# Local attention and whitening on one core: second sums, bias, first band transposes and one weight buffer moved, and the conv weights' loads on another queue

## The chip, the cores and the metric

The kernel runs on one core of one Trainium2 chip. The metric is the device time of one execution in microseconds (us). The engines carry the names that the profile gives them: PE multiplies matrices (PEld is its weight load), DVE does elementwise work and 32x32 block transposes, ACT does activations, scaled copies and copies out of PE's result memory, POOL is GpSimd, and SP issues DMAs. Each engine works through its own list in order. DMAs issued by SP travel on the hardware-driven queue (q1 in the profile), those issued by POOL on the software-driven one (q0).

## The reference, cut to what matters

The input has 4 images of 256 channels and 64 x 64 pixels, in fp32. Two layers follow each other:

```python
# layer 0: attention weights from a dilated 7x7 convolution, then a weighted sum of 49 shifts
k = conv(x, w1, padding=6, dilation=2) + b1          # 256 -> 128 channels, 7 x 7
k = conv(k, w2) + b2                                 # 128 -> 49 channels, 1 x 1
attn = softmax(k, axis=1)
x = einsum('bkchw,bkhw->bchw', the 49 shifts of x by two pixels, attn)
# layer 1: whitening in four groups of 64 channels, by 5 Newton-Schulz steps
mean, Sigma = mean and covariance (+1e-5 I) of each group over all images and pixels
Sigma_N = Sigma / trace(Sigma);  P = I
for _ in range(5): P = 1.5 * P - 0.5 * (P @ P @ P) @ Sigma_N
out = (P / sqrt(trace(Sigma))) @ (x - mean) * weight + bias
```

The statistics of layer 1 need the whole output of layer 0, so all four images go through the attention before the first output is written.

## The kernel before

**The convolution.** The two convolutions are folded into one from 256 channels to 49 (lines 177 to 247). Because of the dilation by two, the four pixel phases of an image are separate small images, and the kernel computes their 7 x 7 convolution by an evaluate, multiply and interpolate scheme in both directions. There are seven evaluation points (EVAL), of which the rows 1 to 5 and the columns 1 to 5 are combinations with small factors; point 0 and the point INF at infinity read the image directly. For one image and one row point `br`, `row_eval` (L437) makes the row's combination on DVE in one of three buffers `rb`; `col_ops` (L471) makes from it the column points `xh`; `conv_bank` (L518) multiplies them with the transformed weights on PE in three banks (BANKS: points 1, 2, 0, then 3, 4, INF, then 5), 96, 80 and 32 profiled matmuls of 0.275 us, and copies each bank to `pv` on ACT (L546); `col_interp` (L615) interpolates on DVE into `zz`. After the last row `row_interp` (L641) interpolates over the rows and adds the bias on ACT (L658), which gives the logits. Image 0 takes rows 1, 2 and 3 like this, and its rows 0, 4, 5 and INF by direct sums on PE (`direct`, L662, 56 profiled matmuls, 11.6 us); images 1 to 3 take rows 0 to 5 by `conv_bank` and INF by a direct sum.

A direct sum for a row that carries two weight rows comes in two parts. The part `s == 0` is copied to `zz`. The part `s == 1` is one row lower; its last row is copied on ACT (L690) and the rest is added on DVE (L691).

**The weights.** `weights` (L364) makes the transformed weights of one row and bank the first time that they are wanted, on DVE with copies and scalings on ACT or POOL, stores them in memory (`gd`, L434), and loads them from there for each later image (L378), 45 loads in all: 588, 490 and 196 KB for the banks 0, 1 and 2. Each bank has one buffer (tags wr0 to wr2), so a load waits until the matmuls of the same bank of the row before have read it. Rows 4 and 5 have their row combination parked in memory (`kept`); it is loaded for image 1 into `rb[0]` (L387), from which that row's weights are then made.

**The attention.** `softmax(b, pc)` (L849) works on one column parity: PE turns the logits (L859), DVE takes the maximum (L865), ACT the exponentials (L873), DVE scales (L886). An attention block n = 4b + 2h + pc then goes through memory: `move_terms` (L895) copies its terms to `zt` (L919) and stores them to `sd` (L932); `load_band` (L952) reads them back as a banded matrix in three parts, each with four DMAs (L960), and transposes each part in place on DVE (L973). `make_block` (L985) turns the image on PE, `weighted_sum` (L1009) multiplies it with the band (L1020), `store_y` (L1030) writes the result over the image (ACT L1039), and `turn_y` and `moments` gather the covariance (L1052, L1060, L1073).

**Memory.** Five image slots stand for eight half images. Images 1 and the first half of image 2 are loaded by `load_x` (L126) on POOL's queue; later `move` (L1086) spills a finished slot to memory (L1091) and loads the next half image into it (two DMAs of 1 MB, L130), also on POOL.

**The order.** `conv_step` (L719) runs one bank and at once prepares the same bank of the next row. Blocks of attention of the image before are put between the steps by a plan with eight gaps per image (L1171 to L1226). PE's instructions keep the order of the program (`pe`). On the other engines and on the queues a scheduler orders instructions when the program is built, by priority and by when it takes them to be ready. `tc.high_priority()` raises a priority; `add_manual_dep` with NoSync fixes an order without a wait; `in_turn` and `in_order` chain DVE's instructions strictly, throughout image 0's convolution and around the last rows of the others. `later` is a list of final copies that are put behind the ACT copy of the next bank 1 (L550 to L560).

Of the kernel before, what the change touches and what calls it, by code (L numbers as in the profile page):

```python
# [10 lines left out]
AF = mybir.ActivationFunctionType  # L11
# [21 lines left out]
def kernel(  # L33
# [330 lines left out]
    def weights(b, br, i, mid=None):  # L364

        first = (br, i) not in made  # L370
        made.add((br, i))
        s0 = slot_of[BANKS[i][0]]
        ns = sum(len(taps(bc)) for bc in BANKS[i])
        nk = NSK * len(taps(br)) // 2
        wt = apool.tile([P, ns, NSK], F32, tag=f"wr{i}", name=f"wr_{b}_{br}_{i}")[:, :, :nk]
        w = {bc: wt[:, slot_of[bc] - s0 : slot_of[bc] - s0 + len(taps(bc))] for bc in BANKS[i]}
        if not first:
            nc.sync.dma_start(wt, gd[br][:, s0 : s0 + ns])  # L378
            return w

        if br == 0:
            g = [gr0[:, v] for v in range(KS)]
        elif br in kept:

            f = rb[0].rearrange("p q r c w -> p (q r c w)")[:, : KS * nk]
            if i == 0:
                nc.sync.dma_start(f, kept[br])  # L387
            f = f.rearrange("p (v a r k) -> p v a r k", v=KS, a=NCC, k=KT)
            g = [f[:, v] for v in range(KS)]
        else:  # L390
            g = [gbr[:, v] for v in range(KS)]
        g = [t.rearrange("p a r k -> p (a r k)") for t in g]

        e = ct.rearrange("p a b -> p (a b)") if b else store[4].rearrange("p c r w -> p (c r w)")
        e, o, e1 = (e[:, k * nk : (k + 1) * nk] for k in range(3))
        g0 = [g[KS - 1 - a] for a in range(4)]
        g1 = [g[KS - 5 - a] for a in range(3)]
        o0 = {bc: w[bc][:, 0] for bc in w}
        o1 = {bc: w[bc][:, 1] for bc in w if bc != INF}

        same = nc.scalar.copy if b == 0 else nc.gpsimd.tensor_copy
        if i == 0:
            add(e, g0[0], g0[2])
            add(o, g0[1], g0[3])
            add(e1, g1[0], g1[2])
            add(o0[1], e, o)
            sub(o0[2], e, o)
            add(o1[1], e1, g1[1])
            sub(o1[2], e1, g1[1])
            same(o0[0], g0[0])  # L410
            same(o1[0], g1[0])
        elif i == 1:
            madd(e, g0[2], 4.0, g0[0])
            madd(o, g0[3], 4.0, g0[1])
            madd(e1, g1[2], 4.0, g1[0])
            madd(o0[3], o, 2.0, e)
            madd(o0[4], o, -2.0, e)
            madd(o1[3], g1[1], 2.0, e1)
            madd(o1[4], g1[1], -2.0, e1)
            same(o0[INF], g0[3])  # L420
        else:
            madd(o0[5], g0[0], 2.0, g0[1])
            madd(o1[5], g1[0], 4.0, g1[2])
            madd(o0[5], o0[5], 2.0, g0[2])
            if mid is not None:
                mid()
            madd(o1[5], g1[1], 2.0, o1[5])
            madd(o0[5], o0[5], 2.0, g0[3])
            add(o1[5], o1[5], o1[5])
        for bc in BANKS[i]:  # L430
            f = SCALE[bc] * (SCALE[br] if br not in kept else 1.0)
            if f != 1.0:
                nc.scalar.mul(w[bc], w[bc], f)
        nc.sync.dma_start(gd[br][:, s0 : s0 + ns], wt)  # L434
        return w
# [205 lines left out]
    def row_interp(b, part):  # L641

        pt = {k: zz[:K2, k] for k in range(NP)}
        lg = lgx
        if b == 0:
            lg = store[4].rearrange("p c r w -> p (c r w)")
        lg = lg[:, : SH * W].rearrange("p (r w) -> p r w", w=W)
        outs = phases(lg[:K2])
        cut = lambda t, k: t[:, k : k + Q8]
        tr = ct.rearrange("p a b -> p (a b)")[:K2, : Q9 * W].rearrange("p (q w) -> p q w", w=W)  # L650
        interpolate(pt, tr, outs, cut, part)
        if part == 0:
            done_ = ((0, outs[0]), (2, outs[2]))
        else:
            done_ = ((3, cut(pt[5], 0)), (1, outs[1]))
            logits[b] = lg
        for a, t in done_:
            nc.scalar.activation(outs[a], t, AF.Identity, bias=bias[:K2])  # L658

    logits = {}  # L660

    def direct(b, br, s, ps, w, xr=None):  # L662


        a = 3 if br == INF else 0
        order = [(v, cc) for v in sorted(range(KS), key=lambda v: abs(v - R)) for cc in range(NCC)]
        for j, (v, cc) in enumerate(order):
            d = 2 * (v - R)
            w0, w1_ = max(0, -d), min(W, W - d)
            for h in range(2):  # L670
                if xr is None:
                    xs = slots[2 * b + h].rearrange("p c (q a) w -> p a q c w", a=4)[:, a]
                else:
                    xs = xr[:, :, h]
                pe(
                    nc.tensor.matmul(  # L676
                        ps[h * HB : h * HB + KT, :, w0:w1_],
                        w[v][:, cc],
                        xs[:, :, cc, w0 + d : w1_ + d],
                        start=(j == 0),  # L680
                        stop=(j == len(order) - 1),
                        skip_group_check=True,
                    )
                )
        z = zz[:K2, br]
        if s == 0:
            with tc.high_priority():
                nc.scalar.copy(z[:, :Q8], ps[:K2])
        else:
            nc.scalar.copy(z[:, Q8], ps[:K2, Q8 - 1])  # L690
            add(z[:, 1:Q8], z[:, 1:Q8], ps[:K2, : Q8 - 1])  # L691

    def conv_psum():
        ncv[0] += 1
# [102 lines left out]
    for i in three:  # L797
        bank(2, i)
    row_weights(4)
    keep_weights(4)  # L800
    xrs[4] = row_eval(0, 4)
    direct0(4, 0)
# [46 lines left out]
    def softmax(b, pc):  # L849

        lv = logits[b].rearrange("p r w -> p (r w)")
        nm = f"{b}_{pc}"
        mx = work.tile([P, NCH, 2], F32, tag="mx", name=f"mx_{nm}")
        lt = []
        for hf in range(2):
            lt.append(tp().rearrange("p (i h k) -> p i h k", i=NI, h=2))
            for i in range(NI):
                pe(
                    nc.tensor.transpose(  # L859
                        lt[hf][:, i].rearrange("p h k -> p (h k)")[:, :K2],  # L860
                        lv[:K2, bass.ds(2 * (NI * hf + i) * P + pc, P, 2)],
                        ident[:K2, :K2],
                    )
                )
            nc.vector.tensor_reduce(  # L865
                mx[:, NI * hf : NI * (hf + 1)], lt[hf][:, :, :, :KT], AX.X, ALU.max
            )
        nc.vector.tensor_scalar(mx, mx, -1.0, None, ALU.mult)  # L868
        d = terms[b, pc] = bpool.tile([P, 2, NCH, KT], F32, tag="d", name=f"d_{nm}", bufs=2)
        s = work.tile([P, 2, NCH], F32, tag="s", name=f"s_{nm}")  # L870
        for h in range(2):
            for i in range(NCH):
                nc.scalar.activation(  # L873
                    d[:, h, i], lt[i // NI][:, i % NI, h, :KT], AF.Exp,
                    bias=mx[:, i, h : h + 1], accum_out=s[:, h, i : i + 1],
                )
            nc.vector.reciprocal(s[:, h], s[:, h])
            rm = work.tile([P, NCH, KS], F32, tag="rm", name=f"rm_{nm}_{h}")
            nc.vector.tensor_tensor(
                rm,  # L880
                s[:, h].unsqueeze(2).to_broadcast([P, NCH, KS]),
                cmask.unsqueeze(1).to_broadcast([P, NCH, KS]),
                ALU.mult,
            )
            dh = d[:, h].rearrange("p i (u v) -> p i u v", u=KS)
            nc.vector.tensor_tensor(  # L886
                dh, dh, rm.unsqueeze(2).to_broadcast([P, NCH, KS, KS]), ALU.mult
            )

    terms, moved, loaded = {}, set(), set()  # L890

# [57 lines left out]

    BAND = ((0, 3), (3, 5), (5, 8))  # L950

    def load_band(n, part):  # L952

        if (n, part) in loaded or n not in moved:
# [4 lines left out]
        for g in range(CR):  # L959
# [6 lines left out]
                ),  # L966
            )

        f = band.rearrange("p m r w -> p (m r) w")[
            :, m0 * BP + (R if m0 == 0 else 0) : m1 * BP - (R if m1 == NCH else 0)  # L970
        ].rearrange("p e w -> p (e w)")
        with tc.high_priority():
            nc.vector.transpose(f, f)  # L973
        if (n, part) == (4 * B - 1, len(BAND) - 1):
            bring_back(dma)

# [199 lines left out]

    def soft(b, pc):
        with tc.high_priority() if pc == 0 else nullcontext():
            softmax(b, pc)
        soft_done.add((b, pc))  # L1180
        if pc == 0:
            bands(4 * b)
# [263 lines left out]
```

## Time and profile before

| | us |
|---|---|
| median of 3 runs | 752.98 (752.46 to 753.97) |
| the profiled execution's time | 753.07 |
| its span, first to last instruction | 751.3 |
| DVE idle in the span (751.3 less 611.5 busy) | 139.8 |
| PE matmuls of the banks (L536), 4368 | 249.7 |
| PE matmuls of the weighted sums (L1020), 640 | 154.6 |
| SP's queue waiting at the weights' loads (L378) for PE | 135.9, in 26 waits |
| SP's queue waiting at the band loads (L960) for PE y | 69.9, in 22 waits |
| POOL waiting at the spills (L1091) for ACT | 127.3, in 3 waits |

The mean granted PE clock is 0.984. The chain that ended last is made of 60% PE, 27% DVE, 5% ACT, 4% DMA and 3% issue. Roughly, the span has the folding of the weights until 29 us, image 0's convolution until 157, image 1's with the attention of image 0 beside it until 300, the same for images 2 and 3 until 578, the rest of the attention until 682, the whitening matrices until 698, and the output.

How to read it: busy time is an engine's own; time in which an engine waits costs only where the others wait for it in turn. In a timeline a line gives start, duration, engine, source line, operation, what is written and read, the number of merged instructions, and in brackets the idle time before it and what ended it. L313, L306 and L309 are helpers (multiply-add, add, subtract), so their lines are told apart by tile names. In the windows' view the columns are the stretch, its length, the busy time and number of instructions of PE, PEld, DVE, ACT and POOL, then the granted PE clock, the DMA share and GB/s.

### The profile page before, as it was taken

Reading aid. Unit: us, or ns where it says so; the run is one execution under the profiler, and the core shown is the slowest. Engines: PE = TensorE matmul, PEld = TensorE weight load, DVE = VectorE, ACT = ScalarE, POOL = GpSimd, SP = SyncE. Lnnn points to the kernel's source line nnn. Section 1 sums busy time; section 2 is a strip of 40 time slices with the busy share of each in tenths; the row PEclk is TensorE's granted clock in tenths of the full one; section 3 lists DMA queues with packets and bytes.
Section 4 is the critical chain, followed back from the end, with each engine's and each line's share of the span. In section 5 each row is a group of like instructions: output and inputs, shape, how many; then the busy total and the mean of one; then the engine's idle time right before and its main releaser. Section 6 shows DMA issues by size and latency. Waiting matters only on the chain.

```text
span 751.3 us, 18491 instructions
## 1 busy us (share of the span) xinstructions
PE 706.7 (94%) x7512; PEld 531.5 (71%) x7512; DVE 611.5 (81%) x1268; ACT 332.3 (44%) x953; POOL 50.9 (7%) x52
## 2 busy tenths in 40 slices
PE   6999999997988997999999999999999889998996
PEld 1449643376887795599998976899998678885331
DVE  3799899998999988877997799799969665545575
ACT  1424240253564354375453443745435573322564
POOL 0410070020000110001000100000000000000000
PEclk9999999999999998999999999999999999999999
DMA  8981120127153393046743930433532243362588
GB/s 322 257 302 73 60 88 17 64 98 232 64 183 120 103 342 97 21 132 217 256 130 116 336 82 1 146 111 110 166 90 82 50 135 111 117 251 118 209 359 327
DMA packets 59629, 114.41 MB, mean 152 GB/s; under 512 B 22887, under 2 KB 42008, under 8 KB 58776
## 3 DMA queue, kind: packets, MB, share of 16 engines
q1 hardware_dynamic: 55848, 94.36, 37.7%
q0 software_dynamic: 3696, 18.88, 7.3%
q8 instruction: 59, 0.97, 0.5%
q14 instruction: 26, 0.21, 0.1%
HBM read 65.88 MB, written 47.33 MB: 151 GB/s over the span
## 4 chain that ended last, share of the span: by engine, by line
PE 60%; DVE 27%; ACT 5%; DMA 4%; issue 3%; SPq 1%; DVEq 0%; ACTq 0%
PE cv L536 18%; PE y L1020 13%; PE acc L676 6%; PE tp L1386 4%; PE sig L1073 3%; PE tp L1052 3%; PE cv L676 3%; PE tp L991 3%; DVE xh L313 3%; DVE pv L313 2%; DVE rb L313 2%; DVE zz L313 2%; DMA band<-sd 2%; DVE band L973 2%; PE cv L222 2%
## 5 line engine op out<-in xcount | busy, mean ns | idle before, releaser
L536 PE MATMUL cv<-xh,wr 128*49 128x128 f32 x4368 | 249.7, 275 | 5.9 <-DVE xh L306 5.6
L536 PEld LDWEIGHTS cv<-xh,wr 128*49 128x49 f32 x4368 | 243.6, 124 | 9.9 <-issue 7.1
L1020 PE MATMUL y<-band,xb 128*128 128x224 f32 (+2 forms) x640 | 154.6, 381 | 8.7 <-ACT xb L999 6.7
L1020 PEld LDWEIGHTS y<-band,xb 128*128 128x128 f32 x640 | 111.4, 196 | 31.4 <-ACT xb L999 9.4
L546 ACT COPY pv<-cv 113x486 f32<-113x486 f32 (+1 forms) x63 | 30.0, 476 | 84.6 <-PE cv L536 84.4
L1039 ACT ACTIVATE slot<-y,pivot 128x512 f32<-128x512 f32 x53 | 36.7, 740 | 67.5 <-PE y L1020 67.4
L1060 ACT COPY yt<-tp 128x256 f32<-128x256 f32 x128 | 45.5, 379 | 37.8 <-PE tp L1052 36.4
L973 DVE STREAM_TRANSPOSE band<-band 128x864 f32<-128x864 f32 (+1 forms) x48 | 47.6, 992 | 13.2 <-DMA band<-sd 13.1
L991 PE MATMUL tp<-ident,slot 128*128 128x128 f32 x256 | 50.0, 297 | 8.2 <-ACT yt L1060 8.2
L313 DVE SCALAR_TENSOR_TENSOR pv<-pv 113x162 f32<-113x162 f32 x186 | 55.2, 320 | 0.8 <-ACT pv L546 0.3
L1052 PE MATMUL tp<-ident,slot 128*128 128x128 f32 x256 | 52.0, 299 | 3.7 <-ACT yt L1060 1.0
L1052 PEld LDWEIGHTS tp<-ident,slot 128*128 128x128 f32 x256 | 41.2, 205 | 13.8 <-issue 4.0
L991 PEld LDWEIGHTS tp<-ident,slot 128*128 128x128 f32 x256 | 40.1, 205 | 14.8 <-ACT yt L1060 9.7
L873 ACT ACTIVATE d<-tp,mx 128x49 f32<-128x49 f32 x128 | 36.9, 337 | 21.4 <-DVE mx L868 17.9
L919 ACT COPY zt<-d 32x112 f32<-32x112 f32 (+2 forms) x156 | 44.8, 287 | 1.9
L313 DVE SCALAR_TENSOR_TENSOR xh<-ct 128x512 f32<-128x512 f32 x42 | 27.9, 685 | 13.7 <-PE cv L536 13.4
L1073 PEld LDWEIGHTS sig<-yt 128*64 128x64 f32 x1024 | 33.2, 140 | 6.4 <-issue 4.9
L1073 PE MATMUL sig<-yt 128*64 128x65 f32 x1024 | 37.7, 228 | 0.0
L999 ACT COPY xb<-tp 128x256 f32<-128x256 f32 x87 | 30.5, 375 | 14.0 <-PE tp L991 13.4
L999 DVE COPY xb<-tp 128x256 f32<-128x256 f32 x41 | 16.4, 421 | 23.4 <-PE tp L991 23.4
L676 PE MATMUL acc<-slot,tap 128*49 128x496 f32 (+3 forms) x168 | 34.6, 569 | 0.0
L873 ACT ACTIVATION_READ_ACCUMULATOR d<-tp,mx 128x1 f32 x128 | 30.8, 242 | 0.0
(222 smaller groups left out, 958.0 us busy)
## 6 DMA issues: line engine op xcount, KB each, us to landing
out_dram<-out SPq DMA_DIRECT2D x32, 512.0 KB, 3.4
sd<-zt SPq DMA_DIRECT2D x16, 896.0 KB, 4.0
slot<-in_x_dram POOLq DMA_DIRECT2D x12, 1024.0 KB, 10.1
band<-sd SPq DMA_DIRECT2D x128, 84.0 KB, 2.1
wr<-gd SPq DMA_DIRECT2D x15, 588.0 KB, 3.7
wr<-gd SPq DMA_DIRECT2D x15, 490.0 KB, 4.0
spill<-slot POOLq DMA_DIRECT2D x3, 2048.0 KB, 7.7
back<-spill SPq DMA_DIRECT2D x3, 2048.0 KB, 13.1
```

The costliest lines, as they stand in the source:

```text
L313: return in_turn(STT(o, a, f, b, ALU.mult, ALU.add))
L536: nc.tensor.matmul(cv[h * HB : h * HB + KT, k, sr : sr + n, sc : sc + n], wv[:, sc, sr, cc], xh[bc][:, :n, h * NCC + cc, :n], start=(j == ...
L676: nc.tensor.matmul(ps[h * HB : h * HB + KT, :, w0:w1_], w[v][:, cc], xs[:, :, cc, w0 + d : w1_ + d], start=(j == 0), stop=(j == len(order) ...
L873: nc.scalar.activation(d[:, h, i], lt[i // NI][:, i % NI, h, :KT], AF.Exp, bias=mx[:, i, h : h + 1], accum_out=s[:, h, i : i + 1],)
L919: ins = nc.scalar.copy(o, i)
L973: nc.vector.transpose(f, f)
L991: nc.tensor.transpose(t[:, cc * P : (cc + 1) * P], xt[:, cc, CR * m : CR * (m + 1), bass.ds(pc, SW, 2)], ident,)
L999: (nc.vector.tensor_copy if tail else nc.scalar.copy)(xb, t[:, :C])
L1020: nc.tensor.matmul(ps[:, cc, q0 - half * HALF : q1 - half * HALF, :], xb[:, cc * P : (cc + 1) * P], rhs, start=(k == 0), stop=(k == len(PI ...
L1052: nc.tensor.transpose(t[:, cc * P : (cc + 1) * P], yt[:, cc, CR * i : CR * (i + 1), bass.ds(pc, SW, 2)], ident,)
L1060: nc.scalar.copy(yb.rearrange("p a g c -> p (a g) c")[:, :, :GW], t[:, :C].rearrange("p (e c) -> p e c", c=GW),)
L1073: nc.tensor.matmul(sig[g * GW : (g + 1) * GW, cc], yb[:, cc, g, :GW], yb[:, cc, g], start=(count[0] == 0 and cc == 0), stop=(count[0] == 4 ...
```

## The change

It has five parts.

1. In `weights` the 45 loads of finished weights are issued by POOL (`nc.gpsimd`) and no longer by SP.
2. For row 5 the parked combination is loaded into `lgx` (the buffer that later holds the logits of images 1 to 3, and before held image 0's row 0 weights) and no longer into `rb[0]`.
3. The second part of image 0's row 0 sum (L690 and L691) is put into a list `seconds` and run after the banks of row 3 and `row_weights(4)`.
4. In `row_interp` for images 1 to 3 the two bias activations of part 0 go into `later`, so they are put behind ACT's copy of bank 1 of row 5.
5. For block 0 `load_band` issues its DMAs but keeps the three transposes in a list `held`; they are issued after softmax (0, 1), each with an order behind that softmax's last DVE instruction.

```diff
@@ weights
         if not first:
-            nc.sync.dma_start(wt, gd[br][:, s0 : s0 + ns])
+            nc.gpsimd.dma_start(wt, gd[br][:, s0 : s0 + ns])
             return w
...
-            f = rb[0].rearrange("p q r c w -> p (q r c w)")[:, : KS * nk]
+            f = lgx if br == 5 else rb[0].rearrange("p q r c w -> p (q r c w)")
+            f = f[:, : KS * nk]
@@ row_interp
         for a, t in done_:
-            nc.scalar.activation(outs[a], t, AF.Identity, bias=bias[:K2])
+            def end(a=a, t=t):
+                return nc.scalar.activation(outs[a], t, AF.Identity, bias=bias[:K2])
+            if b > 0 and part == 0:
+                later.append(end)
+            else:
+                end()
@@ direct
         else:
-            nc.scalar.copy(z[:, Q8], ps[:K2, Q8 - 1])
-            add(z[:, 1:Q8], z[:, 1:Q8], ps[:K2, : Q8 - 1])
+            def second():
+                nc.scalar.copy(z[:, Q8], ps[:K2, Q8 - 1])
+                add(z[:, 1:Q8], z[:, 1:Q8], ps[:K2, : Q8 - 1])
+            if br == 0:
+                seconds.append(second)
+            else:
+                second()
@@ image 0
     for i in three:
         bank(2, i)
     row_weights(4)
+    seconds.pop()()
     keep_weights(4)
@@ softmax: the last tensor_tensor (L886) is returned as last
@@ before load_band
+    held = []
+    def release_held(after):
+        for f in held:
+            tc.add_manual_dep(
+                f().ins, after.ins.name,
+                mybir.DependencyInfo(mybir.DependencyClass.NoSync, mybir.DependencyReason.DATA),
+                reason="release_held",
+            )
+        held.clear()
@@ load_band
-        with tc.high_priority():
-            nc.vector.transpose(f, f)
+        def turn_blocks():
...
+            with tc.high_priority():
+                return nc.vector.transpose(f, f)
+        if n == 0:
+            held.append(turn_blocks)
+        else:
+            turn_blocks()
@@ soft
-            softmax(b, pc)
+            last = softmax(b, pc)
+        if pc == 1:
+            release_held(last)
```

## The prediction

> **What bounds the kernel now.** I read the page's busy shares first, then the chain of waits by stretch, then the timelines of DVE, PE, ACT, SP and POOL where the chain leaves PE, and the granted clock in windows.
>
> ```profile
> PE 706.7 (94%) x7512; PEld 531.5 (71%) x7512; DVE 611.5 (81%) x1268; ACT 332.3 (44%) x953; POOL 50.9 (7%) x52
> ```
>
> PE is busy 94% of the span, so a step pays only where PE waits or where DVE, which then sets the pace, waits. From 300 to 575 us PE idles hardly at all: what has been gained or lost by 300 us is carried to the end. The losses lie before it:
>
> ```profile
> 86.55 0.62 DVE L306 TENSOR_TENSOR zz<-zz,acc 113x448 f32<-113x448 f32 x1 [3.58 <-ACT zz L690]
> ...
> 183.17 1.08 DVE L973 STREAM_TRANSPOSE band<-band 128x864 f32<-128x864 f32 x1 [2.82 <-DMA band<-sd]
> ...
> 286.34 1.08 DVE L973 STREAM_TRANSPOSE band<-band 128x864 f32<-128x864 f32 x1 [2.90 <-DMA band<-sd]
> ```
>
> Three DVE stalls: the strictly ordered add of the second sum waits for its matmuls; twice a band transpose, put at the head of DVE, waits for its DMA. PE answers:
>
> ```profile
> 188.72 6.99 PE L536 MATMUL cv<-xh,wr 128*49 128x128 f32 x96 [5.59 <-DVE xh L306]
> ...
> 290.20 0.50 PE L991 MATMUL tp<-ident,slot 128*128 128x128 f32 x2 [3.76 <-ACT yt L1060]
> 290.54 0.51 PE L1052 MATMUL tp<-ident,slot 128*128 128x128 f32 x2
> 291.60 6.12 PE L1020 MATMUL y<-band,xb 128*128 128x320 f32 x12 [0.55 <-ACT xb L999]
> ```
>
> After an idle PE comes a half-speed PE; the twelve y matmuls take 6.12 us here and 3.18 elsewhere in the chain (332.42). In the windows' line the column before the last two is the clock:
>
> ```profile
> 290.40:298.00 7.60, 7.05 (x27) 4.56 (x28) 7.60 (x19) 2.22 (x7) 0.00 (x0) 0.55 0.00 0
> ```
>
> Why the second band DMA is late (8.5 us from issue to landing, 2.1 in the median of its row) is in SP's timeline and the queues' traffic in 274 to 280 us:
>
> ```profile
> 272.53 0.32 SPq L378 DMA_DIRECT2D wr<-gd  x1
> 274.26 0.32 SPq L434 DMA_DIRECT2D gd<-wr  x1
> 276.08 2.12 SPq L960 DMA_DIRECT2D band<-sd  x4
> ```
> ```profile
> DMA packets 563, 2.03 MB, mean 339 GB/s; under 512 B 33, under 2 KB 125, under 8 KB 561
> ...
> q0 software_dynamic: 324, 1.26, 61.1%
> q1 hardware_dynamic: 237, 0.75, 38.2%
> ```
>
> POOL's two image loads (q0, issued 270.86, 1 MB each) fill the engines, and on SP's own queue a weights' load of 588 KB, not needed before 319.6, goes ahead of the band (336 KB in four).
>
> **What the Trainium skill says.** "DMA: Bandwidth & Descriptors", Queues, rings and completion order: an engine takes each ring's descriptors in order and goes round robin between rings. That fits the 61 to 38% above, and means that weights on POOL's queue no longer stand before the bands but behind images. The same page, Issuing engines are not separate DMA queues: another issuing engine brings no bandwidth; so I count order only. "SBUF — State Buffer", Who interferes with whom: DVE in a two-port mode locks GpSimd out, so descriptors are late. The trace shows none: POOL's twelve image issues take 1682 to 1816 ns beside whatever DVE does (a POOL copy, L410 at 97 us, does take 13.99 us). "TensorE: Matmul & The Clock Gate", Part 1: an idle PE falls to half clock and needs about 3.4 us of work to recover; the windows (0.54 to 0.58 after the idles at 183, 234, 254 and 286) agree.
>
> **The change part by part.** Sums are against the profiled run: 753.07 us, span 751.3, so 1.8 us around it; the median of three runs is 752.98, and I take the difference to that.
>
> *Second sum later.* Nothing is removed. ACT's edge copy (0.22) and DVE's add (0.62) of row sum 0 go behind the third row's banks and row_weights(4). DVE no longer idles 3.58 us at 83. It then runs ahead, but PE works on until 97.85 and had idled only 0.93 us for DVE's rb (ready 98.63). From 98.78 PE has five sums of 11.6 us in a row, and DVE waits at the next add (122.9) the longer. Gain 0.9. Without that PE cover it would be 3.6.
>
> *Held transposes.* The three of block 0 (1.08 + 0.83 + 1.07) go behind the last multiply of soft(0,1). DVE no longer waits 2.82 at 180.34. What was queued behind: the rest of an interpolation, mx L868, for which ACT waited 8.1 us with its exps, and the xh that PE awaited until 188.72. All these move up by 2.82 plus the transposes in front of them (1.08 to 1.9), so PE starts that bank near 184. The transposes still run, near 188 to 191; y of block 0 (196.7 before) is their first reader, and PE has a bank of 5.5 us before it. DVE is then busy to 241 (24.9 and 24.4 of each 25 us), so its 2.82 us carry; PE's larger advance is lost again where it waits for DVE. Gain 2.8. That bank's weights were issued at 184.25 on SP, behind twelve band loads; alone on SP they would have landed near 188 and kept the gain small. On POOL they can go at 176.7, when their buffer comes free.
>
> *Weights' loads on POOL.* 45 issues of 0.34 leave SP (15 us); POOL gets 45 of about 0.57 (spill, the nearest row: 128 long rows), 26 us on an engine busy for 51. Each waits for the bank before it on the same buffer; behind it in POOL's order may stand spills, image loads and the three weight copies of rows 4 and 5. Landing was 3.7 us in the median; I take 4 to 5 on POOL (estimate: the same bytes and an issue 0.2 longer), up to 12.6 behind an image. The weights land mostly 7 to 19 us before use, so this is free; tightest were 0.14 (176.51 to 176.64) and 2.5 us. The former's buffer is free at 167.85, but SP stood until 170.97 behind the sd store: 3 us better on POOL. Gain: near 276 us 0.60 MB goes from before the band. At q1's 0.75 MB in 6 us that is 4.8 us: the band lands near 281.4, DVE asks for it at 283.44, the 2.90 us stall is gone. Next late is ACT: its bias (288.02) follows DVE's lgx and everything behind it moves up 3.0 us, PE's restart from 290.2 to 287.2. Gain 3.0, bounds 0 (the images alone hold the band) and 7.7 (all 4.3 us of idle and 3.4 of half clock saved).
>
> *Row 5's weights in lgx.* The load at L387 waited for rb (244.62) and landed at 248.88; lgx is free from 156. POOL's copies and DVE's first adds of that row (250.5) can come up to 2 us earlier, so ACT's scaling at 252.78, on which xb and the y matmuls at 256.1 hang, may too. PE lost 1.2 us and 1.7 of clock there. I take 0; bounds 0 and 2.9.
>
> *Late bias.* Two ACT instructions of 0.72 per image go behind the second bank's copy of row 5. In image 1 the second one (288.02) stood behind that copy (284.10) already, so nothing; in images 2 and 3 PE does not idle there. Taken 0, bounds -0.7 and +0.7.
>
> Sum: 0.9 + 2.8 + 3.0 = 6.7 us, so 752.98 - 6.7 = 746.3.
>
> **Rivals.** *More: the clock stays up as well.* If PE's gaps become short, the half-clock stretches at 189, 256 and 290 (1.7 + 1.7 + 3.4) go, and row 5's 1.2: 14 us, 739. For it: a gap of 1.79 us at 210.7 cost no clock. Against: 1.23 at 254.9, with smaller ones, did.
>
> *Less: the band is late anyway.* The two images alone hold q1 to a share; or PE and ACT give the 2.8 back before 300. Then 0.9 + 2.8 or less: about 750. For it: the band transfer among 896-byte packets; against: the wide share of weights ahead of it.
>
> *Nothing:* the new order of DVE and ACT adds waits as large as those removed, about 753.
>
> *Slower: weights queued behind the image loads.* POOL works in order. At 337.29 it issues a spill, then waits until 353.55 for the loads of the next image, which land at 364.4. The weights of three banks become ready at 340.2, 345.6 and 350.1; if the compiled order puts the image first, the first of them (196 KB) lands near 365 where its matmuls start at 357.65: 7.5 us of idle PE and 1.7 of clock. The same at 418.8: images landing at 433.1, weights at 434.8, use at 431.42: 3.4. First alone: 9.2 - 6.7, so 755.5; both and a second half clock, near 760. It decides once an image is issued ahead of a weights' load that is used within about 12 us of the issue. For it: POOL's long waits.
>
> ```profile
> 337.29 0.57 POOL L1091 DMA_DIRECT2D spill<-slot  x1 [63.05 <-ACT slot L1039]
> 353.55 3.37 POOL L130 DMA_DIRECT2D slot<-in_x_dram  x2 [15.70 <-PE tp L991]
> ```
>
> Against it: the waits concerned, except on spills, all end on PE instructions whose order is fixed, so an order made by readiness should keep the weights first.
>
> **How the numbers follow.** Forecast 0.39 (own range 743 to 749), more 0.10, less 0.15, nothing 0.08, slower 0.28. A fifth of "less" is within 0.2% (1.5 us, about what a measurement of this kernel can tell from no change). So faster 0.61, same 0.11, slower 0.28. The range, 741 to 758, leaves out half of "more" and a third of "slower".
>
> **What would show it.** DVE without idle time before zz<-zz,acc near 83 and before the transposes near 181 and 284; the xh bank of 188.7 near 183 to 184; band loads landing within 5 us near 276; clock near 1.0 where the windows have 0.55. PE idle before cv matmuls with a weights' DMA as releaser, or POOL waiting on an image with weights behind it, would prove me wrong; so would an advance at 300 us that is absent at 420.

## The result, and the profile after

The changed kernel takes 754.58 us in the median of 20 runs (751.34 to 765.04). The kernel before, timed beside it, takes 751.49 (749.40 to 753.97, 20 runs). The ratio is 1.0026, with a 95% interval of 1.0013 to 1.0040: 2 us slower (3.1 by the medians), where 6.7 us faster was forecast. The one execution of 765.04 us was in a slow state of the chip and is not in the ratio.

The profiled execution of the changed kernel took 752.20 us with a span of 750.4, that of the kernel before 753.07, so this pair alone would show 0.9 us faster. Four more executions were profiled at the end (experiments 13, 14, 17 and 18). They show that the first one of before was unlike the others at 256 us, and that both kernels end in one of several ways; so the stretch up to 300 us is compared with the second execution of before (752.84).

By the page PE is busy for 701.9 us after (706.7 before), DVE for 611.0 (611.5) and POOL for 88.1 (50.9). POOL has 37 us more than before. 45 issues of about 0.55 us are 25 of them; one copy accounts for the rest. The windows' view tells the stretches apart (length, then busy time of PE, PEld, DVE, ACT and POOL, the clock, the DMA share, GB/s). After, then the second execution of before:

```profile
157.00:221.00 64.00, 60.23 (x909) 56.67 (x906) 63.90 (x129) 34.86 (x135) 10.39 (x16) 1.00 0.58 174
221.00:296.00 75.00, 57.49 (x682) 51.21 (x683) 62.09 (x148) 31.28 (x77) 21.85 (x12) 0.91 0.42 142
```
```profile
157.00:221.00 64.00, 55.59 (x787) 51.77 (x788) 60.91 (x121) 32.93 (x130) 6.44 (x7) 0.97 0.45 136
221.00:296.00 75.00, 67.26 (x851) 60.12 (x845) 69.99 (x164) 34.26 (x85) 10.30 (x9) 0.93 0.53 177
```

In the first stretch PE gains: it is busy for 60.23 us against 55.59 before, at full clock. In the second it loses: 57.49 against 67.26. From 300 us to the end of the attention at 682 the two kernels run alike: in their first executions PE's busy time agrees to within 0.3 us in each stretch.

PE's timeline of the changed kernel has the gain and the two losses:

```profile
183.23 5.53 PE L539 MATMUL cv<-xh,wr 128*49 128x128 f32 x96 [1.35 <-DVE zz L313]
...
210.89 10.02 PE L539 MATMUL cv<-xh,wr 128*49 128x128 f32 x176
...
228.85 5.53 PE L539 MATMUL cv<-xh,wr 128*49 128x128 f32 x96
236.07 6.48 PE L539 MATMUL cv<-xh,wr 128*49 128x128 f32 x112 [1.68 <-POOL wr L413]
...
251.22 5.53 PE L1062 MATMUL y<-band,xb 128*128 128x320 f32 x12 [6.10 <-ACT xb L1041]
...
260.98 7.27 PE L539 MATMUL cv<-xh,wr 128*49 128x128 f32 x128
...
287.47 3.24 PE L539 MATMUL cv<-xh,wr 128*49 128x128 f32 x32 [9.14 <-DVE xh L313]
```

The kernel before, second execution, at the same places:

```profile
188.71 6.95 PE L536 MATMUL cv<-xh,wr 128*49 128x128 f32 x96 [5.69 <-DVE xh L306]
...
218.37 10.02 PE L536 MATMUL cv<-xh,wr 128*49 128x128 f32 x176
...
239.86 11.80 PE L536 MATMUL cv<-xh,wr 128*49 128x128 f32 x208
...
255.75 3.18 PE L1020 MATMUL y<-band,xb 128*128 128x320 f32 x12 [1.24 <-ACT xb L999]
...
263.16 7.27 PE L536 MATMUL cv<-xh,wr 128*49 128x128 f32 x128
...
296.66 1.93 PE L676 MATMUL cv<-slot,pv 128*49 128x512 f32 x8
```

The reader sees the advance of the changed kernel grow from 5.5 us (188.71 less 183.23) to 11.0 (239.86 less 228.85), fall to 4.5 at the twelve y matmuls (255.75 less 251.22) and, because these take 5.53 us instead of 3.18 (the clock is 0.81 in 244 to 262 us, and 1.00 in the second execution of before), to 2.2 behind them (263.16 less 260.98), and turn into a delay of 1.8 at the direct sum of image 2 (296.66, against 298.41 to 299.09 in three executions of the changed kernel). 8.8 us are lost in the first place, low clock included, 3.9 in the second. That the end lies within 2 us of the kernel before is chance: an advance of 11.0 us and losses of 12.7 happen to be of one size.

*The first place.* POOL's and SP's timelines of the changed kernel:

```profile
221.32 14.70 POOL L413 COPY wr<-rb 128x196 f32<-128x196 f32 x1 [18.84 <-PE tp L1094]
```
```profile
214.92 1.96 SPq L390 DMA_DIRECT2D rb<-g4d  x1
236.33 0.32 SPq L437 DMA_DIRECT2D gd<-wr  x1
236.75 1.82 SPq L995 DMA_DIRECT2D band<-sd  x3
```

The copy of a plain part of row 4's weights took 14.70 us. It is the one that took 0.35 us at 228.72 before, where DVE was at a band transpose (228.51 to 229.58), which has one input. What it reads is the parked row in `rb`. SP issued the load of that row at 222.42 before and issues it at 214.92 now. That is no more than the advance: in both kernels the load goes out 4.0 us behind the start of the bank of 176 matmuls on PE (218.37 and 210.89), and the copy begins 10.3 to 10.4 us behind it. What has moved against PE is DVE, here by its third band transpose of the block (after, then before in its first execution, which is here within 0.02 us of the second):

```profile
217.41 1.07 DVE L1010 STREAM_TRANSPOSE band<-band 128x864 f32<-128x864 f32 x1
```
```profile
228.51 1.07 DVE L973 STREAM_TRANSPOSE band<-band 128x864 f32<-128x864 f32 x1
```

It comes 6.5 us behind the bank's start instead of 10.1, and the first add of row 4's weights 12.0 instead of 14.7. So the copy no longer falls under the transpose but into a dense stretch of DVE instructions with two inputs. On SP the store of these weights (L437) waits for the copy, and the band loads of the next block stand behind that store, until 236.75. On DVE their transpose is at the head:

```profile
235.12 0.68 DVE L313 SCALAR_TENSOR_TENSOR xh<-xh,rb 128x512 f32<-128x512 f32 x1
242.51 1.08 DVE L1010 STREAM_TRANSPOSE band<-band 128x864 f32<-128x864 f32 x1 [6.70 <-DMA band<-sd]
```

DVE's last instruction before its idle time ends at 235.80, and the copy ends at 236.02. Behind the transpose stand the adds of row 5's weights. ACT waits 5.77 us for them before its scaling at 249.47, the block's `xb` stand behind that scaling, and PE waits 6.10.

*The second place.* DVE after, DVE in the second execution of before, and the queues' section for 272 to 284 us after:

```profile
283.67 1.08 DVE L1010 STREAM_TRANSPOSE band<-band 128x864 f32<-128x864 f32 x1 [3.53 <-DMA band<-sd]
...
286.64 0.68 DVE L313 SCALAR_TENSOR_TENSOR xh<-xh,rb 128x512 f32<-128x512 f32 x1
```
```profile
279.44 0.68 DVE L313 SCALAR_TENSOR_TENSOR xh<-xh,rb 128x512 f32<-128x512 f32 x1
...
284.33 1.08 DVE L973 STREAM_TRANSPOSE band<-band 128x864 f32<-128x864 f32 x1 [2.94 <-DMA band<-sd]
```
```profile
q0 software_dynamic: 613, 2.57, 66.0%
q1 hardware_dynamic: 736, 1.05, 24.9%
...
band<-sd SPq DMA_DIRECT2D x4, 84.0 KB, 7.8
```

The first band part of block 3 lands 7.8 us after its issue (8.6 in the section for 274 to 280 us before), so taking the weights' load from SP's queue bought 0.8. That load is still beside the band: POOL issues its 588 KB at 270.12, behind the two images and ahead of the band's loads (271.84 to 275.7), and it takes 12.5 us to land. In this order the last multiply-add of `xh` for column point 5 stands behind the waiting transpose; before it stood ahead. PE waits 9.14 us for that `xh`, and then runs at half clock.

### The profile page after: what moved, and what is told of

It is laid out like the page before. It is cut to its first block, busy times and chain, and to the rows that moved or that the text cites. A ratio compares the mean times of both kernels' runs of the same rounds, so it can differ in the third digit from the quotient of the medians.

```text
span 750.4 us, 18511 instructions
## 1 busy us (share of the span) xinstructions
PE 701.9 (94%) x7512; PEld 528.6 (70%) x7512; DVE 611.0 (81%) x1268; ACT 332.2 (44%) x953; POOL 88.1 (12%) x97
## 4 chain that ended last, share of the span: by engine, by line
PE 61%; DVE 25%; ACT 6%; DMA 3%; issue 2%; POOL 2%; SPq 0%; DVEq 0%; ACTq 0%
PE cv L539 20%; PE y L1062 12%; PE acc L686 6%; PE tp L1430 4%; PE tp L1094 3%; PE cv L686 3%; PE sig L1115 3%; PE tp L1033 3%; DVE pv L313 2%; DVE zz L313 2%; DVE xh L313 2%; DVE ct L313 2%; PE cv L222 2%; POOL wr L413 2%; DMA band<-sd 2%
## 5 line engine op out<-in xcount | busy, mean ns | idle before, releaser
L539 PE MATMUL cv<-xh,wr 128*49 128x128 f32 x4368 | 249.7, 275 | 12.5 <-DVE xh L313 9.1
L539 PEld LDWEIGHTS cv<-xh,wr 128*49 128x49 f32 x4368 | 243.3, 124 | 16.7 <-issue 10.4
L1062 PE MATMUL y<-band,xb 128*128 128x224 f32 (+2 forms) x640 | 151.7, 376 | 12.9 <-ACT xb L1041 11.1
L379 POOL DMA_DIRECT2D wr<-gd x45 | 24.3, 540 | 278.9 <-PE cv L539 258.8
```

The source lines that it names most:

```text
L539: nc.tensor.matmul(cv[h * HB : h * HB + KT, k, sr : sr + n, sc : sc + n], wv[:, sc, sr, cc], xh[bc][:, :n, h * NCC + cc, :n], start=(j == ...
L1062: nc.tensor.matmul(ps[:, cc, q0 - half * HALF : q1 - half * HALF, :], xb[:, cc * P : (cc + 1) * P], rhs, start=(k == 0), stop=(k == len(PI ...
```

## The experiments

They have the numbers of their labels (e1 is experiment 1). The first twelve were timed over five rounds beside the kernel before, on the same chip for those sent together. Medians are given with the ratio to the kernel before; two experiments are compared by the difference of their ratios times 752 us. Such a difference is uncertain by 2 to 3 us.

**1. The three copies on ACT** (ACT has already made them for image 0):

```diff
-        same = nc.scalar.copy if b == 0 else nc.gpsimd.tensor_copy
+        same = nc.scalar.copy
```

> The changed kernel with the three plain copies of a row's weights on ACT instead of POOL, for all images. Copy theory (a POOL copy of row 4's weights is held 14.7 us at 221 by DVE's two-input stream; through SP's in-order queue it delays the gd stores, the band loads, DVE at 235.8 (6.70) and PE at 245 (6.10)): no copy over 1 us, the DVE stall near 236 and the PE stall near 245 under 2 us each, time 745 to 749, ratio to before 0.992 to 0.997. Queue theory (the weights' loads on POOL cost it): time stays at 753 to 756. Order theory (the held transposes' new DVE order costs it, PE idle 9.14 at 278): the stall at 236 may go, the one at 278 stays at 8 to 9 us, time 751 to 753.

745.97 us, ratio 0.9924 (0.9895 to 0.9954), 7.7 us better than the change. The stalls at 236 and 245 are gone (PE's is 1.06). The stall near 278 stays:

```profile
278.30 3.65 PE L539 MATMUL cv<-xh,wr 128*49 128x128 f32 x32 [8.79 <-DVE xh L313]
```

The time is what the copy theory gave; experiment 7 leaves open whether up to 3.0 of the 7.7 us come with copies on ACT in any kernel. The queue theory, in which the loads on POOL cost the time in themselves, is out. The stall at 278 is a second cause.

**2. The weights' loads back on SP** (parts 2 to 5 alone):

```diff
-            nc.gpsimd.dma_start(wt, gd[br][:, s0 : s0 + ns])
+            nc.sync.dma_start(wt, gd[br][:, s0 : s0 + ns])
```

> The changed kernel with the weights' loads back on SP; parts 2 to 5 alone. Copy theory: the load of row 4's parked combination moves back behind SP's weights' loads to about 222, so the copy starts later or the same as in the kernel before; time 747 to 751, and the long POOL copy at 221 is gone or ends by 236. Queue theory: 746 to 748. Order theory: 751 to 755 with the PE stall of 9 us near 278 still there.

748.26 us, ratio 0.9939 (0.9917 to 0.9962). The load of the parked row went out at 219.57, not near 222 as the copy theory had it, and the copy is short all the same (0.66 us at 225.97), though DVE is at multiply-adds with two inputs there too. PE does not wait 9 us near 278, so the order theory, which laid that stall on the held transposes, is out: it comes with part 1. What is left of PE's stall at 181 is here a wait of 5.96 us for weights, until 187.74 (in experiment 15, which is the same kernel, the wait is 5.29 and DVE's `xh` comes last).

**3. Part 1 alone,** the same line changed in the kernel before:

> The kernel before with the weights' loads on POOL alone (part 1 alone). Copy theory: row 4's parked combination is loaded early on SP, its copy on POOL runs against DVE's stream for over 10 us, time 752 to 757. Queue theory: slower than before by 2 to 5 us without a long copy. Order theory: 748 to 750, the 3 us that the prediction gave to this part.

762.75 us, ratio 1.0143 (1.0111 to 1.0175): 10.8 us slower than the kernel before, worse than any theory gave. It has the long copy (13.50 us at 227.40), both stalls (7.57 us before the twelve y matmuls at 257.57, and the line below), and the one at 188 that part 5 removes:

```profile
293.06 3.66 PE L536 MATMUL cv<-xh,wr 128*49 128x128 f32 x32 [8.13 <-DVE xh L313]
```

**4. Part 5 undone:**

```diff
-        if n == 0:
+        if False:
             held.append(turn_blocks)
```

> The changed kernel with block 0's transposes issued at once (part 5 undone). Copy theory: the stall at 181 returns (2.8 us of DVE, 5.6 of PE), the long copy near 221 stays, time 755 to 759. Order theory: the PE stall near 278 falls from 9.14 to under 4 us, time 750 to 753.

759.21 us, ratio 1.0094 (1.0068 to 1.0119). Part 5 is worth 5.1 us here. The long copy (14.40) and PE's 7.96 near 285 to 293 are there without it.

**5. Copies on ACT, and one transpose with its usual priority:**

```diff
-            with tc.high_priority():
+            with nullcontext() if (n, part) == (3, 0) else tc.high_priority():
                 return nc.vector.transpose(f, f)
```

> As e1_copies_act, and the transpose of the first part of block 3's band without raised priority, so that on DVE it stands behind the last multiply-adds of row 5's column point 5 (xh) and no longer ahead of them. Turn theory (with the weights' loads off SP the scheduler puts this transpose ahead of xh, and its band lands 8 us after its issue beside 2 MB of image loads, so that PE waits 8.8 us at 269 to 278): PE's stall near 278 falls to under 4 us, time 740 to 744, ratio 0.984 to 0.990. Ring theory (the band is late in any order and the time is lost there): the wait moves to y behind the transpose, time stays at 745 to 747.

740.66 us, ratio 0.984 (0.9812 to 0.9869): 12 us faster than the kernel before and 14 than the change. The turn theory holds and the ring theory falls. The four band loads still take 7.3 us in the median, but nothing waits for them: `xh` goes first, and the transpose follows with no idle time ahead of it (DVE's timeline, then PE's):

```profile
272.66 0.69 DVE L313 SCALAR_TENSOR_TENSOR xh<-xh,rb 128x512 f32<-128x512 f32 x1
...
275.14 1.07 DVE L1010 STREAM_TRANSPOSE band<-band 128x864 f32<-128x864 f32 x1
```
```profile
273.50 3.01 PE L539 MATMUL cv<-xh,wr 128*49 128x128 f32 x32 [4.04 <-DVE xh L313]
```

The direct sum of image 2 begins at 284.70, 12.0 us ahead of the second execution of the kernel before.

**6. Parts 2 to 5 with the copies on ACT** (the edits of 1 and 2 together):

> Parts 2 to 5 (the weights' loads on SP) with the copies on ACT. Copy theory: the 12.8 us copy at 95 was the only long one left in e2_loads_sp and delayed nothing, so 746 to 749, as e2_loads_sp. If copies on ACT gain by themselves: 741 to 745. Part 1 is then worth the difference to e1_copies_act, 745.97: minus 2 to plus 4 us by the turn theory, plus 3 by the prediction.

746.80 us, ratio 0.9928 (0.9900 to 0.9956), the same as experiment 2. So where no copy that SP waits for is shut out, moving it to ACT brings nothing. Against experiment 5, part 1 is worth 6.6 us once its two costs are repaired; this is an upper bound, since the late transpose was not tried with the loads on SP, where PE still waits 3.05 us near 282.

**7. The kernel before with the copies on ACT:**

> The kernel before with the copies on ACT, as a control. Copy theory: there the copies of rows 4 and 5 on POOL took 0.35 us each and only the one at 97 took 14, which delayed nothing that the end waits for: 751 to 753, no gain over 1.5 us. If copies on ACT gain by themselves: 745 to 749, and e1_copies_act says nothing of the change.

751.05 us, ratio 0.9960 (0.9936 to 0.9984). That is 1.8 us by the medians and 3.0 by the ratio, more than the copy theory allowed and less than the other case. Its profiled execution, 756.12, is far from its median, so no trace tells where this came from; row 5's copy, which took 3.5 us in two of three executions of the kernel before, is a candidate and not shown.

**8. Part 1 alone with both repairs** (the edits of 1 and 5 on experiment 3):

> The kernel before with part 1 alone, the copies on ACT, and the transpose of block 3's first band part without raised priority. If the long copy and the early transpose are the whole cost of part 1: 748 to 752, at or below the kernel before. If the queue itself costs: 754 to 758.

748.35 us, ratio 0.9930 (0.9905 to 0.9954). From 1.0143 the repairs bring 16 us. Against experiment 7 part 1 alone, with the late transpose, gains 2.3, which is within the uncertainty. The loads on POOL's queue thus cost nothing that can be measured in themselves.

**9. Four short pauses for DVE,** copies on POOL as in the change. After row 4's bank 0 weights, four times, each ordered behind the one before:

```diff
             sub(o1[2], e1, g1[1])
+            if b and br == 4:
+                for _ in range(4):
+                    nc.vector.memset(pause, 0.0)
```

> The changed kernel, with four DVE memsets of 128x224 (about 0.2 us each, no SBUF input, nobody reads them) behind the multiply-adds of row 4's bank 0 weights; the copies stay on POOL. Copy theory (DVE instructions with two SBUF inputs, back to back, keep the POOL copy out until the first gap): the copy that began at 221 ends within 1 us of the first memset, near 225 to 226 instead of 236, the two others follow by 229, the DVE stall near 236 and the PE stall near 245 are under 3 us, time 745 to 750, although DVE has 0.9 us more to do. If the copy is slow for another cause (its load, POOL's own queue): it stays at 13 to 15 us, time 753 to 757.

742.73 us, ratio 0.9874 (0.9854 to 0.9895). DVE has 0.96 us more to do and the kernel is 11.4 us faster than the change. POOL's timeline, then DVE's:

```profile
221.46 3.48 POOL L425 COPY wr<-rb 128x196 f32<-128x196 f32 x1 [19.25 <-PE tp L1106]
224.88 1.37 POOL L426 COPY wr<-rb 128x196 f32<-128x196 f32 x1
226.20 0.84 POOL L435 COPY wr<-rb 128x196 f32<-128x196 f32 x1
236.26 12.20 POOL L425 COPY wr<-lgx 128x196 f32<-128x196 f32 x1 [9.22 <-issue]
```
```profile
224.73 0.24 DVE L417 MEMSET pause<- 128x224 f32 x1
224.87 1.18 DVE L306 TENSOR_TENSOR ct<-rb 128x1024 f32<-128x1024 f32 x1
226.04 0.24 DVE L417 MEMSET pause<- 128x224 f32 x1
226.18 0.65 DVE L306 TENSOR_TENSOR xh<-ct 128x512 f32<-128x512 f32 x1
226.83 0.24 DVE L417 MEMSET pause<- 128x224 f32 x1
```

Each copy ends 0.21 us after the start of one memset: 224.94, 226.25 and 227.04, against starts of 224.73, 226.04 and 226.83. Between two memsets, under 1.18 us of DVE's add, the second copy does not end. Up to the first memset DVE's order here is that of the change, so it is the memset that ends the long copy; this is the mechanism, seen three times in a row. The gain of 11.4 us is not all of it, because the memsets also changed the scheduler's order further on. In the second execution (experiment 16) SP issues the band loads of the second place at 267.54, 9.4 us behind the image loads instead of 5.1; they land in 5.3 us instead of 7.8, the transpose waits 1.54 us instead of 3.53, one instruction and not three stands between it and `xh`, and PE waits 2.77 us at 276.62. In this first profiled execution, at 746.88 the longest of five (the others 742.3 to 743.0), row 5's first copy was held 12.20 us at 236.26, and PE then waited 9.40 us.

**10. The late transpose alone,** copies on POOL (the edit of 5 without that of 1):

> The changed kernel with only the transpose of block 3's first band part put behind xh (copies on POOL as in the change). Turn theory and copy theory together: the PE stall near 280 falls from 9.14 to about 4, the copy of 14 us and the PE stall near 245 stay; with the two costs independent time is 754.6 less 5.3 = 749 to 750; if the one hides the other, 752 to 755.

747.80 us, ratio 0.9924 (0.9894 to 0.9953), 7.7 us better than the change. The two costs add, within the uncertainty: 7.7 and 7.7 singly, 14.0 together. In its profiled execution, 743.96, DVE happened to wait 0.73 us for PE after 231.56, and the copy that began at 222.79 ended at 231.76, after 8.97 us. PE's stalls are 3.12 us at 247.74, where 6.10 was expected to stay, and 4.60 at 278.64, where about 4 was expected.

**11. Experiment 5 with part 5 undone** (the edit of 4):

> e5_act_late_turn (740.66) with block 0's transposes not held (part 5 undone): the prediction gave part 5 2.8 us, so 743 to 744; e4_not_held against the changed kernel showed about 4.6, so 745 to 746.

745.73 us, ratio 0.9914 (0.9889 to 0.9939). Part 5 is worth 5.6 us in the repaired kernel, as against the change.

**12. Experiment 5 with parts 2 and 4 undone** (`rb[0]` for row 5 again, the bias at once):

> e5_act_late_turn (740.66) with parts 2 and 4 undone (row 5's parked weights in rb[0] again, the bias of part 0 at once). The prediction gave both nothing: 740 to 742. If the buffer or the bias is worth its upper bound, 743 to 745.

740.37 us, ratio 0.9843 (0.9825 to 0.9861). The two together are worth nothing that can be measured.

**13 to 18. Further executions, profiled, of four kernels unchanged:** the changed one (13, 14), those of experiments 2 and 9 (15, 16), the kernel before (17, 18).

> The changed kernel once more, to see a second and further executions of it. If its times lie in two groups (near 752 and near 755.5) because of the copies: an execution near 755 has a second copy of over 5 us (row 5's, near 240) or a PE stall near 245 that is 3 us longer than 6.10, and one near 752 has not. If because of the first image loads: DVE's wait near 39 us is some 3 us longer than 3.45 in the executions near 755, and the copies are alike. In both cases the copy near 221 takes over 8 us each time.

> As e13_after_again, the third profiled execution of the changed kernel: copies differ between executions near 752 and 755.5, or the wait near 39 us does; the copy near 221 takes over 8 us again.

> The kernel of e2_loads_sp once more. There the three copies of row 4 took 0.66, 0.81 and 0.81 us at 226, beside DVE multiply-adds with two SBUF inputs. If the order of the work decides who gets through: under 1 us each again. If it is chance: one over 5 us may appear.

> The kernel of e9_four_pauses once more. Its one profiled execution, 746.88, was 4 us above its other four and had row 5's first copy held 12.2 us at 236. If that copy made the difference: an execution near 742.5 has row 5's copies under 2 us. Each of row 4's three copies again ends about 0.2 us after the start of one memset.

> The kernel before once more, profiled, to see which of its times (median 751.49, its first profiled execution 753.07) come from where. Its copies: 14 us near 97 and 0.35 near 229 again, if the order of the work decides. The direct sum of image 2, at 299.41 in the first, within 0.5 us if the spread comes from the end of the kernel, and 1 to 2 us earlier in an execution near 751 if it comes from the part before 300.

> As e17_before_again, the third profiled execution of the kernel before: copies of 14 us near 97 and 0.35 near 229 again; the spread of its times from the part before 300 us or from the end of the kernel.

Times: 753.73, 752.88, 748.49, 743.24, 752.84 and 753.32 us. The copy of row 4 takes 14.45 and 14.63 us in the changed kernel, 0.35 both times in the kernel before, and 0.70, 0.81 and 0.80 in that of experiment 2. So for this copy the order of the work decides, not chance. With the pauses, each of the three ends 0.21 us after the start of a memset again. Row 5's first copy takes 0.61 there instead of 12.20 (its third 7.99), PE waits 3.97 us instead of 9.40 for the bank behind it, the direct sum of image 2 begins at 286.63 instead of 290.52, and the execution is 3.6 us shorter. For row 5's copy, then, the order does not decide, and in this one pair it makes the difference.

Neither case that was named for the two groups of the changed kernel's times holds: the copies are alike, and so is PE at the direct sum (298.41, 298.43, 299.09), with or without DVE's wait of 3.45 us at 39 us. The difference is at the end of the kernel, in the whitening matrices. In 692 to 704 us the clock is 1.00 in the changed kernel's first execution (752.20) and 0.86 in its second (753.73). The kernel before has both ways too: 1.00 in its first execution, 0.86 in the two others. From POOL's copies to `swap` (585 to 588 us) to the end it takes 163.2 to 163.3 us in the one way and 164.8 to 166.0 in the other, in both kernels. It is no part of the change.

The first execution of before, at the direct sum only at 299.41, had half a clock at 256 us (0.91 in 244 to 262 us) where experiment 18 has 1.00. In experiments 17 and 18 the direct sum begins at 296.66 and 297.06. So the changed kernel is 1.3 to 2.4 us behind at 300 us, about what the ratio says.

## Why the prediction was wrong, step by step

**Second sum later (0.9): right in kind.** DVE no longer idles at 83, and it waits longer at the next add, 3.46 us near 121.7 in experiments 1 and 5. The price was not tried by itself.

**Held transposes (2.8): right in mechanism, too small in size.** Experiments 4 and 11 give 5.1 and 5.6 for part 5. The mis-sized term is "its 2.82 us carry; PE's larger advance is lost again where it waits for DVE". PE's bank began at 183.23, within the 183 to 184 that was named, and the advance was not lost again: it grew to 11.0 us by 228.85 (parts 1 and 5 together). The condition in the same paragraph was right. With the loads on SP the bank waits for its weights (5.96 us in experiment 2, 5.62 in experiment 6), and parts 1 and 5 pay in full only together.

**Weights' loads on POOL (3.0): here the prediction failed,** at "The weights land mostly 7 to 19 us before use, so this is free". Part 1 alone costs 10.8 us. The loads themselves are as free as was said (experiment 8); the rival "weights queued behind the image loads", to which the prediction gave its 0.28, has the right sign and the wrong mechanism. Nearest in number and in kind is the rival *Nothing*, "the new order of DVE and ACT adds waits as large as those removed", which was given 0.08. The failing step put at nothing what happens once the loads have left SP's queue, above all a new order on DVE:

- In the change and in experiments 3 and 4, which have the loads on POOL, DVE's third band transpose of the block comes 6.3 to 6.6 us behind the start of PE's bank, and the first add of row 4's weights 11.8 to 12.1. In the kernel before it is 10.1 and 14.7, in experiment 2 8.6 and 13.6. The load of the parked row has not moved against PE: it goes out 4.0 us behind the bank's start in all five. In experiment 4 the copy begins at 228.82, as good as where it began before (228.72), and takes 14.40 us: DVE is there no longer at a transpose but at two-input work, which shuts the copy out. Such a copy had been seen at 97 us with 13.99 us, and was set aside because the image issues were not slowed. The page "SBUF — State Buffer", Who interferes with whom, has the case that matters in another sentence than the one the prediction used: "A DVE instruction with two SBUF inputs contends with a GpSimd instruction that reads SBUF". It also says that the shared ports are an exclusive lock and that issue order decides who blocks. The runs agree as far as this: 0.35 us under a transpose, 8.97 to 14.70 shut out, and done within 0.22 us of the beginning of a gap. They do not agree on the order: in the change 36 DVE instructions that began after the copy went ahead of it. POOL's issue of a weights' load at 270.12 took 0.56 us beside DVE's two-input work.
- At 97 us no cost of the copy was seen. At 221 it stands ahead of a store on SP, and so of four band loads. Cost: 7.7 us (experiment 1 against the change), 8.8 by the trace with the low clock behind the stall.
- "The band lands near 281.4 … the 2.90 us stall is gone" failed twice. The weights' load has changed its queue and not its place in time, and the band gains 0.8 us of the 4.8 that were computed. And DVE's order is not fixed there: with the loads off SP the transpose stands ahead of `xh`, and 3.53 us of DVE become 9.14 of PE. Cost: 7.7 us (experiment 10 against the change), 3.9 by the trace, and 5.3 between the direct sums of experiments 1 and 5 (289.97 and 284.70). That it is the moved loads which make the scheduler put it there is shown by experiments 2 and 3; by which estimate of its own it does so, here and at 221, is not known.

**Row 5's weights in `lgx` and late bias (0 and 0): right** (experiment 12), as a pair. Each by itself was not tried.

**The clock.** The half-clock stretch at 189 went, as its gap went (1.35 us of idle time before 183.23); new ones came behind the new gaps. The rival "the clock stays up as well" at 739 (its terms make 14.7 us, so 738.3) is close to what the repaired kernel does (740.66).

**The test that was named,** "an advance at 300 us that is absent at 420", does not fire. The advance went before 300.

What stays open: what lets a POOL copy through at once beside two-input DVE work. In experiments 2 and 15 three copies took 0.7 to 0.8 us each, one between every two multiply-adds, and in the change one waited through 36 DVE instructions; both repeat. Nor is it settled how the 11.4 us of experiment 9 divide between the short copy and the new order at the second place.

## What to carry to other kernels

When DMAs leave an in-order queue, look at what this does to the order of the engines behind that queue, and at what then runs beside what: measured against PE, the load and the copy at 221 kept their place, and DVE's work moved over them. A short POOL instruction that reads SBUF should not start where DVE runs two-input instructions back to back and an in-order queue waits for it: put it on another engine, or give DVE a pause (with four memsets, 0.96 us, the kernel was 11.4 us faster, though not by the copy alone). And a raised priority fixes no order among instructions: when a transpose waits for a DMA, what the scheduler puts behind it is part of the price of every change upstream.

## What the runs showed of the hardware that was not expected

- A POOL copy of 128x196 that takes 0.35 us under a transpose took 8.97 to 14.70 us beside dense two-input DVE work (row 4's first copy, in six traces), in the change through 36 DVE instructions that each began after it. The thirteen traces with copies on POOL have 26 copies of over 3 us. Of these 23 ended 0.20 to 0.22 us after the first moment at which DVE idled or began a memset with no SBUF input, and three (7.99, 11.88 and 12.20 us) 0.29 to 0.35 us after the beginning of the first transpose. A gap of 0.03 us was enough: in experiment 3 an add ends at 110.84, DVE's next instruction begins at 110.87, and the copy that began at 97.06 ends at 111.04.
- POOL's 45 issues of weights' loads in the change took 0.53 to 0.56 us each. None falls into the stretch in which the copy was held.
- The clock in the whitening stage goes one of two ways in executions of one kernel (1.00 or 0.86 in 692 to 704 us), and with it go 1.6 to 2.8 us; a single pair of profiled executions can hide or feign a difference of that size.
- DVE's wait for the first image varies: 3.45 us at 39 us in the first execution of the change, 7.54 and 6.77 in experiments 7 and 8, none in most. In the change the 3.45 were made up before 183 us.
